# Four graph layers on one core: layer 0's row sums of score tiles, by additions on GpSimd or by accumulating DMAs

## The chip, the cores and the metric

The kernel runs on one core of a Trainium2 chip. The metric is device time in microseconds (us). The kernel before took 1689.95 us, the median of three runs (1689.92, 1689.95, 1690.58). Profiles are of one execution each.

The engines are named as the profile names them: PE is TensorE (PEld its weight loads), DVE VectorE, ACT ScalarE, POOL GpSimd, SP SyncE. SP computes nothing and issues DMAs.

## The reference

The input is a batch of 32 graphs of 512 nodes with 128 features, `x` (32 x 512 x 128), and one adjacency matrix `adj` (512 x 512) of zeros and ones. Four layers follow one another; each normalises `x`, takes the positive part as `h`, and adds its result to `x`. Layer 1 is a gated recurrent step done five times, layer 2 one multiplication by the adjacency, layer 3 three powers of it. The change is in layer 0:

```
x_h  = elu(h @ Wi + bi)
e    = sigmoid(a_tgt[:, :, None] + a_src[:, None, :] + be) * mask     # 512 x 512 scores per graph
agg  = e @ x_h
self = x_h * sum(e, axis=-1, keepdims=True)
out  = concat(elu(concat(agg, self) @ Wn + bn), x_h) @ Wm + bm
```

`mask` is the adjacency with 0.005 in place of its zeros. The sum of each row of `e`, 512 scores, is what the change computes in another way.

## The kernel before, in words

**Tiling.** Everything is held with features or nodes on the 128 partitions and 512 numbers in each, so a tile is 128 x 512 of fp32, 256 KB. A graph's scores are four such tiles, `es[0]` to `es[3]`: source nodes jc x 128 on the partitions, the 512 target nodes along the row. A row sum is thus a sum over partitions and over the four tiles. fp32 matmuls go through PE in two records each; where both operands are rounded to fp32r there is one record, and a value is then split into a rounded part and a remainder, each multiplied on its own.

**Buffers.** `Val` names a value; it takes a slot of a kind when the operation that writes it is ordered: "f" are 36 SBUF tiles of 128 x 512, "q" 4 such tiles of fp32r, "s" 8 small ones, "b" 8 PSUM banks, "m" and "d" places in DRAM. Blocks are transposed by a DVE block transpose, a DMA out to "m" (L384) and a DMA back that puts the blocks elsewhere (L395, L400, L414).

**The order of the work.** Operations of all graphs and layers are listed with `op(engine, us, due, emit, reads, writes, ...)`: an assumed duration, a due time, and `result`, the assumed delay until others see the result. `Plan.order` then runs through assumed time and picks, for each engine, the operation that is ready and due first, if its buffers are free and if it isn't due over 60 us after the oldest one left. The instructions of each engine are issued in that order, so a late operand holds up whatever stands behind it on that engine. POOL's operations and those marked `two` (DVE operations with two SBUF inputs) never overlap in the plan: a flag, `shared`, holds back one while the other runs. Steady graphs are due 56 us apart, and several graphs are in work at a time, in different layers.

The list is planned twice after a test of `adj`. Its zeros and ones are exact in fp32r, so the branch that runs is the one in which adjacency products take two fp32r passes.

**Layer 0 (`layer0`).** For each graph: x_h (L441 with Wi, then an elu of ACT and DVE operations), its products with the weights (L567), the targets' part broadcast to all partitions through DRAM (L591, L594), then for each of the four tiles a tanh on ACT (L619) and (tanh + 1) x mask on DVE (L622). L630 multiplies x_h by the four tiles into the PSUM bank `pn`. The row sums come in one of two ways:

- graphs 0 to 3 (`b < G`, G = 4): four fp32 matmuls with a matrix of ones, one per tile (L441 with ones), summed in PSUM;
- graphs 4 to 31: POOL adds the tiles, `es[0] + es[1]`, `es[2] + es[3]`, and the two sums (L641); ACT rounds the total to fp32r (L647), DVE takes the remainder (L648), and two fp32r matmuls with ones sum both over the partitions (L653).

DVE multiplies x_h by the sums (L656, `own`), L441 with Wn adds that product to `pn`, and an elu and the output product (L666) follow.

**What else is on these queues.** POOL also does one power per layernorm (L478, 128 x 4 numbers), between DVE's statistics (L476) and DVE's L481, after which ACT normalises (L486). SP issues all DMAs: graphs in and out, and the transposes.

Of the kernel before, what the change touches and what calls it, by code (L numbers as in the profile page):

```python
# [14 lines left out]
ALU = mybir.AluOpType  # L15
# [26 lines left out]
class Plan:  # L42
# [13 lines left out]
        self.pieces = {}  # L56
        self.idle = None

    def op(self, eng, us, due, emit, reads=(), writes=(), two=False, keep=0, result=None,
           earliest=0.0):  # L60

        o = Op(eng, us, self.RESULT[eng] if result is None else result, emit, two, keep)
        o.earliest = earliest
        for v in reads:
            o.before.add(v.writer)
        for v in writes:
            o.before.update(v.readers)  # L70
            if v.writer:
                o.before.add(v.writer)
            elif v.kind and v.slot is None:
                o.takes.append(v)
        for v in reads:
            v.readers.append(o)
        for v in writes:
            v.writer, v.readers = o, []
        o.vals = [v.whole or v for v in dict.fromkeys([*reads, *writes])]
        for v in o.vals:  # L80
            v.left += 1
        for v in [*reads, *writes, *o.vals]:
            self.vals[v] = True
        o.before -= {o, None}
        o.due = max([due, *(b.due for b in o.before)])
        for b in o.before:
            b.after.append(o)
        self.ops.append(o)
# [28 lines left out]
    def order(self, end=None):  # L117

        left = [o for o in self.ops if not o.begun]
        for o in reversed(left):  # L120
            o.chain = o.us + max([0.0, *(o.result + a.chain for a in o.after)])
            if end is None:
                o.due = min(o.due, self.last - o.chain)
        by_due, oldest = sorted(left, key=lambda o: o.due), 0
        coming, ready = {e: [] for e in self.until}, {e: [] for e in self.until}
        order, events, index = [], [self.now], {}
        for i, o in enumerate(left):
            index[o] = i
            o.waits = sum(not b.begun for b in o.before)
            o.ready = max([o.earliest, *(self.known(b, o) for b in o.before if b.begun)])  # L130
            if not o.waits:
                heapq.heappush(coming[o.eng], (o.ready, i, o))
                events.append(o.ready)
        events += self.until.values()
        events += [t for f in self.free.values() for t, _ in f] + [self.shared]
        events = [max(t, self.now) for t in events]
        heapq.heapify(events)

        def begins(o, now):
            if o.due > by_due[oldest].due + self.ahead:  # L140
                return False
            if (o.two or o.eng == "POOL") and self.shared > now:
                return False
            keep = 0 if o is by_due[oldest] else o.keep
            if any(v.added and self.clean(now) is None for v in o.takes):
                return False
            return all(
                len(self.free[v.kind]) > keep and self.free[v.kind][keep][0] <= now
                for v in o.takes
            )  # L150

        while events:
            now = heapq.heappop(events)
            if end is not None and now >= end:
                break
            for e in self.until:
                while coming[e] and coming[e][0][0] <= now:
                    _, i, o = heapq.heappop(coming[e])
                    heapq.heappush(ready[e], (o.due, i, o))
                if self.until[e] > now:  # L160
                    continue
                passed, o = [], None
                while ready[e] and o is None:
                    x = heapq.heappop(ready[e])
                    if begins(x[2], now):
                        o = x[2]
                    else:
                        passed.append(x)
                for x in passed:
                    heapq.heappush(ready[e], x)  # L170
                if o is not None and end is not None and any(
                    c.due < o.due and t < now + 0.3 * o.us for t, _, c in coming[e]
                ):
                    heapq.heappush(ready[e], (o.due, index[o], o))
                    o = None
                if o is None and e == "PE" and end is not None and self.idle.known <= now:
                    order.append(self.idle)
                    self.until[e] = now + self.idle.us
                    heapq.heappush(events, self.until[e])
                if o is None:  # L180
                    continue
                order.append(o)
                o.begun = True
                while oldest + 1 < len(by_due) and by_due[oldest].begun:
                    oldest += 1
                o.start, self.until[e] = now, now + o.us
                if o.two or e == "POOL":
                    self.shared = self.until[e]
                for v in o.takes:
                    v.slot = self.free[v.kind].pop(self.clean(now) if v.added else 0)[1]  # L190
                    if v.kind == "b":
                        self.pieces[v.slot] = v.pieces
                o.known = self.until[e] + o.result
                heapq.heappush(events, self.until[e])
                heapq.heappush(events, o.known)
                for v in o.vals:
                    v.left -= 1
                    if not v.left and v.kind:
                        self.free[v.kind].append((o.known, v.slot))
                        self.free[v.kind].sort()  # L200
                for a in o.after:
                    if a in index:
                        a.waits -= 1
                        a.ready = max(a.ready, self.known(o, a))
                        if not a.waits:
                            heapq.heappush(coming[a.eng], (a.ready, index[a], a))
        assert end is not None or len(order) == len(left), "the plan does not end: too few buffers"
        self.now = end or 0.0
        return order
# [3 lines left out]
def tile_four_graph_layers(  # L213
# [27 lines left out]
    nc = tc.nc  # L241
    B, N, D = x.shape
    NC = N // P
    G = 4
# [8 lines left out]
    T_VEC, T_COPY, T_ACT, T_DMA = 0.61, 0.5, 0.6, 0.45  # L253
# [3 lines left out]
    op = plan.op  # L257
# [19 lines left out]
    def at(v):  # L277
        if v.tile is not None:
            return v.tile
        return places[v.kind][v.slot] if v.whole is None else at(v.whole)[:, v.part]  # L280
# [267 lines left out]
    def layer0(b, h, due):  # L548
# [6 lines left out]
        d = due + 6  # L555
        xhT = elu(product(Wi_sb, hT, d, blocks=b >= G), bi_sb, bi_half, d, KEEP)

        d = due + 14
# [23 lines left out]
        d = due + 20  # L582
# [33 lines left out]
        es = []  # L616
        for jc in range(NC):
            e = Val("f")
            op("ACT", T_ACT, d, lambda e=e, jc=jc: nc.scalar.activation(  # L619
                like_tgt(at(e)), of_tgt(), AF.Tanh, bias=at(ends)[:, jc : jc + 1]), [tgt, ends], [e],  # L620
                keep=KEEP if jc == 0 else 0)
# [5 lines left out]
        d = due + 30  # L627
# [3 lines left out]
                at(pn), at(msg)[:, ts(jc, P)], at(es[jc]), start=jc == 0, stop=False),  # L631
                [msg, es[jc]], [pn])

        if b < G:
            ps = Val("b")
            for jc in range(NC):
                product(ones, es[jc], d, ps, start=jc == 0, stop=jc == NC - 1)
        else:
            sums = [Val("f"), Val("f")]
            def add(dst, a, c):  # L640
                op("POOL", 1.6, d - 10, lambda: nc.gpsimd.tensor_tensor(  # L641
                    at(dst), at(a), at(c), op=ALU.add), [a, c], [dst])
            add(sums[0], es[0], es[1])
            add(sums[1], es[2], es[3])
            add(sums[0], sums[0], sums[1])
            high, low, ps = Val("q"), Val("q"), Val("b")
            op("ACT", T_COPY, d, lambda: nc.scalar.copy(at(high), at(sums[0])), [sums[0]], [high])  # L647
            op("DVE", T_VEC, d, lambda: nc.vector.tensor_tensor(  # L648
                at(low), at(sums[0]), at(high).bitcast(F32), op=ALU.subtract),
                [sums[0], high], [low], two=True)  # L650
            def total():
                for n, part in enumerate((low, high)):
                    nc.tensor.matmul(at(ps), at(ones_r), at(part), start=n == 0, stop=n == 1)  # L653
            op("PE", 2 * T_PASS, d, total, [high, low, ones_r], [ps])
# [6 lines left out]
        d = due + 44  # L661
# [16 lines left out]
    def first_layer(b):  # L678
        h = layernorm(b, begin(b))
        layer0(b, h, begin(b))  # L680
# [316 lines left out]
```

## Time and profile before

| | us |
|---|---|
| median of three runs | 1689.95 |
| the profiled execution | 1689.17 |
| its span | 1687.4 |
| POOL additions L641, 84 of them | 129.9 busy, mean 1.548 |
| POOL powers L478, 128 of them | 160.0 busy, mean 1.250 |
| L622 on DVE, 128 of them | 106.2 busy, mean 0.883 (the page leaves it out; from the groups by shape) |
| L653 on PE, 56 records | 24.2 busy, mean 0.512 |
| L441 with ones on PE, 32 records | 15.2 busy, mean 0.593 |
| DMA engines, share of their time | 31.3% |

How to read it: a group's line has the kernel's line, the engine, the operation, what is written and read with its shape, the number of instructions, their busy time and mean, and the engine's idle time just before them with what ended it. Durations of matmuls overlap each other, so PE's pace is read from the chain of waits, which has no overlaps. The granted TensorE clock was 0.999 of full speed.

### The profile page before, as it was taken

To read this page: it belongs to the slowest core of one execution; us is meant where nothing else is said; L and a number is where in the kernel's file an instruction comes from. 1 tells how busy PE (TensorE), PEld (TensorE's weight loads), DVE (VectorE), ACT (ScalarE), POOL (GpSimd) and SP (SyncE) were. 2 spreads that over 40 slices of the span, in tenths; PEclk is the share of its full clock that TensorE was granted. 3 is DMA by queue.
4 is the path that set the end of the run, shared out by engine and by line. 5 is a ranking of instruction groups with operands and counts; after the bars stand their busy time and mean duration, and the time that the engine had idled before them with its cause. 6 is when DMAs were issued, how large, how long until landed. Compare 5 with 4: busy or idle time off the path is not lost.

```text
span 1687.4 us, 21306 instructions
## 1 busy us (share of the span) xinstructions
PE 1667.7 (99%) x6627; PEld 1076.8 (64%) x6627; DVE 1457.7 (86%) x3325; ACT 1127.8 (67%) x2143; POOL 295.8 (18%) x237
## 2 busy tenths in 40 slices
PE   9999999999999999999999999999999999999998
PEld 7555555656666666666666666666666666666797
DVE  6889999999998898889988898889999988877742
ACT  8777676786776676667776677665777766655541
POOL 2121102212122121222202212202222220000110
PEclk9999999999999999999999999999999999999999
DMA  3213333243333332242332433232333333222201
GB/s 107 62 57 101 94 107 94 78 135 95 101 113 101 101 101 85 84 120 95 105 103 77 112 107 92 90 107 88 118 104 99 97 98 94 82 69 88 83 18 52
DMA packets 266875, 156.57 MB, mean 93 GB/s; under 512 B 75392, under 2 KB 235008, under 8 KB 266752
## 3 DMA queue, kind: packets, MB, share of 16 engines
q1 hardware_dynamic: 266752, 155.12, 31.3%
q8 instruction: 54, 0.88, 0.2%
q14 instruction: 69, 0.57, 0.1%
HBM read 82.25 MB, written 72.81 MB: 92 GB/s over the span
## 4 chain that ended last, share of the span: by engine, by line
PE 89%; DVE 6%; ACT 2%; DMA 1%; issue 1%; SPq 0%; DVEq 0%; ACTq 0%
PE b L441 41%; PE b L820 19%; PE b L910 10%; PE b L901 6%; PE b L630 5%; PE b L666 3%; PE b L567 2%; PE b L883 1%; PE b L300 1%; DVE f L845 1%; DVE f L622 1%; DVE r L794 1%; PE b L653 1%; ACT f L486 1%; DVE f L382 1%
## 5 line engine op out<-in xcount | busy, mean ns | idle before, releaser
L478 POOL TENSOR_TENSOR s<-s,nhalf 128x4 f32<-128x4 f32 x128 | 160.0, 1250 | 884.4 <-DVE s L476 840.9
L430 ACT COPY f<-b 128x512 f32<-128x512 f32 x360 | 208.4, 586 | 158.7 <-PE b L820 107.1
L820 PE MATMUL b<-AQ,r 128*128 128x512 f32 x1024 | 302.5, 437 | 1.3 <-DVE r L794 1.3
L820 PEld LDWEIGHTS b<-AQ,r 128*128 128x128 f32 x1024 | 192.2, 188 | 89.9 <-issue 47.4
L845 DVE TENSOR_TENSOR f<-f,b 128x512 f32<-128x512 f32 x320 | 211.6, 676 | 39.8 <-PE b L441 39.1
L446 ACT ACTIVATE f<-f,b4w 128x512 f32<-128x512 f32 x160 | 115.4, 723 | 163.0 <-DVE f L845 160.5
L382 DVE STREAM_TRANSPOSE f<-f 128x512 f32<-128x512 f32 x244 | 205.2, 844 | 21.8 <-ACT f L486 21.3
L910 PE MATMUL b<-r,A_r 128*128 128x512 f32 x768 | 222.8, 426 | 0.0
L486 ACT ACTIVATE f<-x,s 128x128 f32<-128x128 f32 x512 | 210.8, 491 | 17.3 <-DVE s L481 17.2
L641 POOL TENSOR_TENSOR f<-f,f 128x512 f32<-128x512 f32 x84 | 129.9, 1548 | 427.0 <-DVE f L622 299.0
L441 PE MATMUL b<-f,u5T 128*128 128x512 f32 x320 | 163.4, 595 | 6.0 <-DVE f L852 6.0
L910 PEld LDWEIGHTS b<-r,A_r 128*128 128x128 f32 x768 | 139.4, 189 | 46.6 <-issue 24.4
L441 PE MATMUL b<-f,w4T 128*128 128x512 f32 x320 | 163.1, 593 | 2.5 <-ACT f L430 2.5
L441 PE MATMUL b<-f,u3T 128*128 128x512 f32 x320 | 163.3, 593 | 1.7 <-DVE f L866 1.6
L441 PE MATMUL b<-f,w5T 128*128 128x512 f32 x320 | 162.5, 592 | 0.0
L441 PE MATMUL b<-f,w3T 128*128 128x512 f32 x320 | 162.1, 592 | 0.0
L820 PE MATMUL b<-A_r,r 128*128 128x512 f32 x512 | 151.1, 437 | 0.4 <-DVE r L794 0.4
L901 PEld LDWEIGHTS b<-V,f 128*128 128x128 f32 x1024 | 131.8, 191 | 26.3 <-issue 20.1
L862 DVE TENSOR_TENSOR f<-f,f 128x512 f32<-128x512 f32 x160 | 112.9, 707 | 38.0 <-ACT f L446 37.7
L446 ACT ACTIVATE f<-b,b5w 128x512 f32<-128x512 f32 x160 | 109.1, 683 | 53.3 <-PE b L441 52.9
L794 DVE TENSOR_TENSOR r<-f,r 128x512 fp32r<-128x512 f32 x192 | 138.5, 723 | 6.4 <-ACT r L790 6.2
L446 ACT ACTIVATE f<-f,b3w 128x512 f32<-128x512 f32 x160 | 115.0, 720 | 28.8 <-DVE f L845 27.7
(106 smaller groups left out, 2580.5 us busy)
## 6 DMA issues: line engine op xcount, KB each, us to landing
m<-f SPq DMA_DIRECT2D x244, 256.0 KB, 2.1
f<-m SPq DMA_DIRECT2D x184, 256.0 KB, 2.9
f<-m SPq DMA_DIRECT2D x240, 64.0 KB, 2.3
x<-in_x_dram SPq DMA_DIRECT2D x32, 256.0 KB, 3.3
out_dram<-x SPq DMA_DIRECT2D x32, 256.0 KB, 2.4
f<-d SPq DMA_DIRECT2D x28, 256.0 KB, 5.6
f<-in_adj_dram SPq DMA_DIRECT2D x4, 256.0 KB, 3.8
f<-in_L_gnn_weight_dram SPq DMA_DIRECT2D x2, 224.0 KB, 3.3
```

The lines of the kernel that those rows point to most:

```text
L382: op("DVE", us, due, lambda: nc.vector.transpose(view_out(at(blocks)), view_in(at(src))), [src], [blocks])
L430: op("ACT", us, due, lambda: nc.scalar.copy(at(t), at(src)), [src], [t])
L441: nc.tensor.matmul(to, at(w), of, start=start, stop=stop)
L446: op("ACT", us, due, lambda: nc.scalar.activation(at(dst), at(src), AF.Tanh, bias=at(bias), scale=scale), [src, bias], [dst])
L478: op("POOL", 1.35, due, lambda: nc.gpsimd.tensor_tensor(stat(SCALE), stat(VAR), at(neg_half), op=ALU.pow), [s, neg_half], [s])
L486: nc.scalar.activation(at(h)[:, ts(c, P)], at(X[b])[:, c, :], AF.Relu, bias=stat(SHIFT)[:, c : c + 1], scale=stat(SCALE)[:, c : c + 1],)
L641: op("POOL", 1.6, d - 10, lambda: nc.gpsimd.tensor_tensor(at(dst), at(a), at(c), op=ALU.add), [a, c], [dst])
L794: op("DVE", T_VEC, due, lambda: nc.vector.tensor_tensor(part(lo), whole(), part(hi).bitcast(F32), op=ALU.subtract), [src, hi], [lo], two=two)
L820: nc.tensor.matmul(at(pa), at(part)[:, ts(jc, P)], view(at(columns)[:, jc, :]), start=jc == n == 0, stop=jc == NC - 1 and n == PARTS - 1,)
L845: op("DVE", T_VEC, d, lambda: nc.vector.tensor_tensor(at(s), at(u), at(pg), op=ALU.add), [u, pg], [s])
L901: nc.tensor.matmul(at(pz)[:, ts(i, D)], at(hT[i])[:, ts(ic, P)], at(V[k]), start=i == 0, stop=last and i == G - 1,)
L910: nc.tensor.matmul(at(pz), at(adjT)[:, jc, ts(ic, P)], at(part), start=False, stop=jc == NC - 1 and n == PARTS - 1,)
```

## The change

Graphs 2 and 3 sum as graphs 4 to 31 do. And for all of these the four tiles are added otherwise: SP copies `es[0]` to the buffer `sums[0]`, SBUF to SBUF, and POOL issues three DMAs that add `es[1]`, `es[2]` and `es[3]` to it, each after the one before has landed. One "f" buffer is taken in place of two. The plan is told 0.45 us and a delay of 2.6 for the copy, 1.0 us and 3.0 for each accumulating DMA (1.6 and 0.2 for an addition before), and that these DMAs may overlap `two` operations. Since the plan changes, the order of the instructions of all engines changes. With one line more near the top, lines after it are numbered higher by one; in the changed kernel the copy is L641 and the accumulating DMAs are L644.

```diff
-    def op(self, eng, us, due, emit, reads=(), writes=(), two=False, keep=0, result=None,
+    def op(self, eng, us, due, emit, reads=(), writes=(), two=None, keep=0, result=None,
            earliest=0.0):
+        two = eng == "POOL" if two is None else two
         o = Op(eng, us, self.RESULT[eng] if result is None else result, emit, two, keep)
...
-            if (o.two or o.eng == "POOL") and self.shared > now:
+            if o.two and self.shared > now:
...
-                if o.two or e == "POOL":
+                if o.two:
                     self.shared = self.until[e]
...
-        if b < G:
+        if b < 2:
             ps = Val("b")
             for jc in range(NC):
                 product(ones, es[jc], d, ps, start=jc == 0, stop=jc == NC - 1)
         else:
-            sums = [Val("f"), Val("f")]
-            def add(dst, a, c):
-                op("POOL", 1.6, d - 10, lambda: nc.gpsimd.tensor_tensor(
-                    at(dst), at(a), at(c), op=ALU.add), [a, c], [dst])
-            add(sums[0], es[0], es[1])
-            add(sums[1], es[2], es[3])
-            add(sums[0], sums[0], sums[1])
+            sums = [Val("f")]
+            op("SP", T_DMA, d - 10, lambda: nc.sync.dma_start(at(sums[0]), at(es[0])),
+               [es[0]], [sums[0]], result=2.6)
+            for e in es[1:]:
+                op("POOL", 1.0, d - 10, lambda e=e: nc.gpsimd.dma_start(
+                    at(sums[0]), at(e), accum_op=ALU.add), [e, sums[0]], [sums[0]],
+                   two=False, result=3.0)
             high, low, ps = Val("q"), Val("q"), Val("b")
```

## The prediction

> **What bounds the kernel now.** I read the page's busy shares first, then its slices, then the stretches table, and last the timeline around one graph's sum.
>
> ```profile
> PE 1667.7 (99%) x6627; PEld 1076.8 (64%) x6627; DVE 1457.7 (86%) x3325; ACT 1127.8 (67%) x2143; POOL 295.8 (18%) x237
> PE   9999999999999999999999999999999999999998
> DVE  6889999999998898889988898889999988877742
> L641 POOL TENSOR_TENSOR f<-f,f 128x512 f32<-128x512 f32 x84 | 129.9, 1548 | 427.0 <-DVE f L622 299.0
> m<-f SPq DMA_DIRECT2D x244, 256.0 KB, 2.1
> ```
>
> PE is busy in every slice. As a busy PE can be padded by modelled ends, I added its work up at the pace at which the chain of waits steps through it: 0.43 us for each record of an fp32 512-wide matmul, two records per matmul, and 0.23 us for a fp32r one. Over the instruction order that gives 1658 us for a span of 1687.4. So PE is really full; about 20 us are start, end and stalls. POOL is idle four fifths of the time, and removing its work does not by itself shorten anything.
>
> ```profile
> 692.78 0.47 PE b L653 x2
> 693.24 2.58 PE b L441 x6
> ```
>
> These two steps of the chain are the prices: 2.58 / 6 = 0.43 and 0.47 / 2 = 0.235.
>
> ```profile
> 336.00:504.00 168.00, 165.61 (x646) 105.09 (x645) 165.28 (x394) 124.91 (x245) 35.29 (x26) 1.00 0.38 110
> 504.00:1134.00 630.00, 627.53 (x2482) 406.38 (x2481) 557.53 (x1268) 426.52 (x810) 117.58 (x84) 1.00 0.34 98
> ```
>
> The columns are length, then busy time of PE, PEld, DVE, ACT, POOL, then clock, DMA share, GB/s. In the first stretch DVE is as full as PE (165.3 of 168) and PE loses 2.4 us; in the second DVE has 11% to spare.
>
> ```profile
> 680.09 3.59 DVE L622 SCALAR_TENSOR_TENSOR f<-f,mask 128x512 f32<-128x512 f32 x4
> 681.53 1.60 POOL L641 TENSOR_TENSOR f<-f,f 128x512 f32<-128x512 f32 x1 [24.57 <-DVE f L622]
> 683.76 3.03 POOL L641 TENSOR_TENSOR f<-f,f 128x512 f32<-128x512 f32 x2 [0.63 <-DVE f L622]
> 688.84 0.62 ACT L647 CAST q<-f 128x512 fp32r<-128x512 f32 x1
> 690.25 0.68 DVE L648 TENSOR_TENSOR q<-f,q 128x512 fp32r<-128x512 f32 x1
> ```
>
> This is one graph's sum. The four score tiles are done from 680.8 to 683.7, the sums at 686.8; ACT rounds at 688.8, DVE subtracts at 690.25, and PE adds up (L653) at 692.2. Nobody waits long: the order is written so that each step comes just after its operand.
>
> **What the Trainium skill says.** "SBUF — State Buffer", section "SBUF: two separate sides": a DVE instruction with two SBUF inputs and a GpSimd instruction that reads SBUF take turns on one port pair, the loser blocks. The trace agrees: three of these four L622 took 0.69 us and the one that met a POOL addition 1.75; over the run L622 has a mean of 883 ns against that 692, and L641 spreads from 1257 to 4007 ns. "DMA: Bandwidth & Descriptors", section "Two DMAs through the same engine are not ordered": the issuer of a dependent DMA has to wait on the first one's semaphore; the instruction order shows these waits on POOL. The price comes from the same page, section "Anatomy of one DMA — SWDGE (gpsimd) path": about 2.0 us + bytes / 436e3 per GpSimd DMA. No GpSimd DMA is in the trace of before.
>
> **The change part by part.** The sum is made against the profiled execution, 1689.17 us (span 1687.4 and 1.8 around it); the median of 1689.95 is 0.78 above.
>
> *Graphs 2 and 3 leave the matmul with ones.* Two graphs lose four fp32 matmuls (L441 with ones) each and get two fp32r ones (L653): 2 x (4 x 0.86 - 2 x 0.235) = 2 x 2.97 = 5.94 us of PE less. Adding up the changed order at the same prices gives the same, 1658.1 to 1652.2. PE is full also where they lie (before 126 us it idles 1.7 us), so the saving moves all that follows: -5.9. ACT gets 2 x 0.62 and DVE 2 x 0.69 more, over two graphs in which ACT and DVE have 20% to spare: nothing; on PE's path it would be 2.6.
>
> *84 POOL additions go.* POOL's 129.9 us cost nothing where they stood. What they cost is the blocked DVE: 128 x (883 - 692) ns = 24 us of DVE. That only counts where DVE is the limit, in the stretch 336 to 504, where PE lost 2.4 us in all. Bounds 0 and -2.4; I take -1.0.
>
> *30 copies on SP.* Each is one issue of 0.34 us, 10 us in a queue that mostly waits for DVE. It waits for the first score tile, and the block copies of other graphs (L384, L395, L414) are queued behind it; the tile is made by the DVE instruction just before, so nothing: without that cover, the 0.7 us of one L622. Landing: as m<-f, 2.1 us.
>
> *90 accumulating DMAs on POOL, three in a row per graph.* Each waits for the landing of the one before, so three links in series stand where 5.2 us of additions stood. What does a link cost, from wait to landing? From below: a plain copy of this size by SP lands in 2.1. From above: the slowest 256 KB row of the page, f<-d, 5.6. The price of the skill's page gives 2.0 + 0.6 = 2.6 for a plain one, as an estimate. An accumulation reads its destination too: 8 packets of 2 KB per engine at 88 ns (the mean of such packets in this trace) are another 0.7. With 0.3 for the start after a wait I take 3.6.
>
> What is the cover? In the changed order I added up PE's work between the end of a graph's last L630 and its L653: median 13.6 us, against 8.0 before, so the order itself was stretched. The first tile was done 3.7 us before that end in the timeline above. From first tile to L653 there are thus 17.3 us. Needed: copy 2.1 + 3 links + rounding, subtraction and their semaphores 1.8. With 3.6 this is 14.7: hidden, with 2.6 us to spare. PE starts to wait at (17.3 - 3.9) / 3 = 4.5 per link. ACT, which is in order, reaches L647 some 4.5 us before L653 by the PSUM tiles that it reads just before; it starts to wait at (17.3 - 4.5 - 2.1) / 3 = 3.6, exactly my value, and between 3.6 and 4.5 its waiting delays the tanh and copies behind it, which have a microsecond or two of room. So 0 here, but on the edge.
>
> *POOL's queue.* 27 layernorm powers (L478) stand between a graph's first and last sum instruction, against 6 before. Each is queued behind a wait for a landing, and DVE's L481, then ACT's L486, wait for it. At 3.6 the landing is no later than the order allows: 0; if a link is 1 us later, that microsecond goes to DVE's queue in 27 places.
>
> *DMA engines.* 30 copies at 0.7 and 90 accumulations at 1.4 us of all 16 engines are 147 us, on top of the 31.3% of the span: 40%. Late landings get more likely. The chain shows two now (7.8 us m<-f at 257.7, 7.3 us f<-d at 1133.4), in stretches where PE lost 2.6 and 1.5 us. I add one more of that kind: +2.0 (bounds 0 and +10).
>
> Sum: 1689.17 - 5.9 - 1.0 + 2.0 = 1684.2; with 0.78 for the median, **1685.0**.
>
> **Rivals.** *The links are longer than the cover (slower).* At 5.0 us per link the sum is late by 2.1 + 15 + 1.8 - 17.3 = 1.6 us in each of 30 graphs: 48 us, less the 5.9: 1732. It decides from 4.5 on; break-even is at 30 x (3L - 13.4) = 5.9, L = 4.53. At the upper bound of 5.6 it is 30 x 3.4 = 102 us: 1786. For it: three serial round trips, an accumulation that no row shows, ACT already at its edge at 3.6. Against it: SP's copies land in 2.1, and the order leaves 5.6 us more than before.
>
> *The gain is eaten (no change).* Three or four late landings of 1.5 to 2 us each, or powers that come late in POOL's queue, give back the 5.9: 1690. For it: the two late ones of today at 31% DMA share. Against: most of their latency is hidden.
>
> *The change saves no PE time.* If PE had nothing to pull forward in the first 100 us, it would idle where the ones stood: 1690 too. The slices speak against it: PE is full from the start.
>
> **How the numbers follow.** Links within the cover: 0.50, 1685 (1680 to 1688). Gain eaten or not realised: 0.15, 1690. Links over the cover: 0.35, from 1695 to 1786, in the middle 1732. About 0.2% (3.4 us) is what a measurement can tell from no change: below 1686.6 is faster, above 1693.3 slower. Of the first case a little ends within that, of the last too: faster 0.49, same 0.15, slower 0.36. Range: 0.05 lie below 1680 and 0.13 above 1735. The likeliest case's own range is 1680 to 1688.
>
> **What would show it.** Right: PE records of L653 x60 and of ones x16; L622's mean near 0.7 us; an accumulation that lands within 4 us; ACT's idle before the rounding small; PE idle some 15 us in 1680. Wrong: ACT's rounding waiting for a DMA by microseconds per graph, then DVE's subtraction and PE's L653; or L481 waiting for POOL's power; then the links are what I mis-sized.

## The result and the profile after

The changed kernel takes 1678.94 us (median of four runs, 1677.93 to 1680.66) against 1690.18 before (a fourth run added to the three above): a ratio of 0.9936 with a 95% interval of 0.9922 to 0.9949, 11.2 us less. The prediction said 1685.0 with a range from 1680: the direction was right, but the gain is more than twice what was forecast and the time falls below the range. The profiled execution took 1678.16, with a span of 1676.4.

Its page, the lines that answer to those shown of before:

```profile
PE 1662.9 (99%) x6615; PEld 1073.7 (64%) x6615; DVE 1420.3 (85%) x3327; ACT 1130.5 (67%) x2145; POOL 239.6 (14%) x243
PE   9999999999999999999999999999999999999998
DVE  6888999999988888889888898888999988877742
L644 POOL DMA_DIRECT2D f<-f x90 | 80.7, 896 | 536.4 <-DVE f L865 58.1
f<-f POOLq DMA_DIRECT2D x90, 256.0 KB, 3.6
f<-f SPq DMA_DIRECT2D x30, 256.0 KB, 2.3
```

PE's busy time fell by 4.8 us, its idle time (span less busy) from 19.7 to 13.5, and DVE's busy time by 37.4. An accumulating DMA occupies POOL for 0.9 us and lands 3.6 us after its issue; 3.6 was what I had taken for a whole link. The same two stretches, same columns as before:

```profile
336.00:504.00 168.00, 167.43 (x646) 105.96 (x645) 155.07 (x376) 124.10 (x241) 25.55 (x25) 1.00 0.44 123
504.00:1134.00 630.00, 627.99 (x2478) 404.88 (x2477) 546.63 (x1274) 425.38 (x804) 91.39 (x86) 1.00 0.44 119
```

DVE is no longer full in the first of them, and PE loses 0.6 us there in place of 2.4. One graph's sum in the timeline:

```profile
667.40 2.53 DVE L623 SCALAR_TENSOR_TENSOR f<-f,mask 128x512 f32<-128x512 f32 x4 [1.00 <-ACT f L620]
668.12 0.50 SPq L641 DMA_DIRECT2D f<-f  x1
671.10 0.92 POOL L644 DMA_DIRECT2D f<-f  x1 [12.91 <-DMA f<-f]
675.29 0.90 POOL L644 DMA_DIRECT2D f<-f  x1
679.35 0.86 POOL L644 DMA_DIRECT2D f<-f  x1 [3.16 <-DMA f<-f]
683.13 0.62 ACT L648 CAST q<-f 128x512 fp32r<-128x512 f32 x1 [0.93 <-DMA f<-f]
684.42 0.68 DVE L649 TENSOR_TENSOR q<-f,q 128x512 fp32r<-128x512 f32 x1
```

The four mask products take 2.53 us, not 3.59: none of them is lengthened. The copy is issued at 668.12 and its landing lets POOL start 3.0 us later; then the links follow at distances of 4.19, 4.06 and, from the last issue to ACT's rounding, 3.78 us; ACT waits 0.93 us for it. The sum is ready 15 us after the first tile. The 60 distances from one issue to the next in the same graph have a median of 4.13 us (3.8 to 5.3).

### The profile page after: what moved, and what is told of

The parts are those of the page before. It is cut to its first block, busy times and chain, and to the rows that moved or that the text cites. A ratio compares the mean times of both kernels' runs of the same rounds, so it can differ in the third digit from the quotient of the medians.

```text
span 1676.4 us, 21509 instructions
## 1 busy us (share of the span) xinstructions
PE 1662.9 (99%) x6615; PEld 1073.7 (64%) x6615; DVE 1420.3 (85%) x3327; ACT 1130.5 (67%) x2145; POOL 239.6 (14%) x243
## 3 DMA queue, kind: packets, MB, share of 16 engines
q1 hardware_dynamic: 271072, 162.98, 32.5%
## 4 chain that ended last, share of the span: by engine, by line
PE 62%; DMA 2%; DVE 1%; ACT 0%; issue 0%; SPq 0%; DVEq 0%; POOLq 0%
PE b L442 27%; PE b L821 13%; PE b L911 9%; PE b L902 5%; PE b L631 3%; PE b L667 2%; PE b L884 1%; DMA f<-f 1%; PE b L568 1%; DMA m<-f 1%; PE b L654 1%; DMA f<-m 0%; DVE f L383 0%; SPq L420 0%; ACT f L620 0%
## 5 line engine op out<-in xcount | busy, mean ns | idle before, releaser
L479 POOL TENSOR_TENSOR s<-s,nhalf 128x4 f32<-128x4 f32 x128 | 154.8, 1212 | 822.0 <-DVE s L477 702.6
L442 PE MATMUL b<-f,u5T 128*128 128x512 f32 x320 | 163.3, 593 | 1.0 <-DVE f L853 1.0
L442 PE MATMUL b<-f,u3T 128*128 128x512 f32 x320 | 163.3, 593 | 1.0 <-DMA f<-m 1.0
L442 PE MATMUL b<-f,w4T 128*128 128x512 f32 x320 | 162.8, 592 | 0.0
L442 PE MATMUL b<-f,w3T 128*128 128x512 f32 x320 | 162.4, 592 | 0.0
L442 PE MATMUL b<-f,w5T 128*128 128x512 f32 x320 | 162.4, 592 | 0.0
L644 POOL DMA_DIRECT2D f<-f x90 | 80.7, 896 | 536.4 <-DVE f L865 58.1
L863 DVE TENSOR_TENSOR f<-f,f 128x512 f32<-128x512 f32 x160 | 109.2, 683 | 48.9 <-ACT f L447 48.4
L447 ACT ACTIVATE f<-f,b3w 128x512 f32<-128x512 f32 x160 | 114.9, 719 | 43.1 <-DVE f L846 42.2
L795 DVE TENSOR_TENSOR r<-f,r 128x512 fp32r<-128x512 f32 x192 | 130.5, 682 | 12.6 <-ACT r L791 12.4
```

Source lines behind the costliest of these rows:

```text
L442: nc.tensor.matmul(to, at(w), of, start=start, stop=stop)
L447: op("ACT", us, due, lambda: nc.scalar.activation(at(dst), at(src), AF.Tanh, bias=at(bias), scale=scale), [src, bias], [dst])
L479: op("POOL", 1.35, due, lambda: nc.gpsimd.tensor_tensor(stat(SCALE), stat(VAR), at(neg_half), op=ALU.pow), [s, neg_half], [s])
L795: op("DVE", T_VEC, due, lambda: nc.vector.tensor_tensor(part(lo), whole(), part(hi).bitcast(F32), op=ALU.subtract), [src, hi], [lo], two=two)
L863: op("DVE", T_VEC, d, lambda c=c, h=h: nc.vector.tensor_tensor(at(c), at(c), at(h), op=ALU.subtract), [c, h], [c], two=True)
```

## The experiments

Two theories for the 6 us or so that PE's saving doesn't explain: A, DVE is no longer blocked by GpSimd's reads, and I had priced this too low; B, the new order of instructions is better. Fourteen kernels were run, in four sets, each beside the kernel before, which took between 1689.21 and 1689.64 in them.

| kernel | us | ratio to before [95%] |
|---|---|---|
| two graphs only, by additions | 1685.91 | 0.9978 [0.9969, 0.9987] |
| DMAs only, from the fifth graph | 1679.87 | 0.9948 [0.9934, 0.9961] |
| new order, additions | 1694.57 | 1.0030 [1.0019, 1.0041] |
| old order, memsets | 1677.38 | 0.9927 [0.9913, 0.9940] |
| four links | 1809.79 | 1.0711 [1.0692, 1.0729] |
| tree | 1690.99 | 1.0011 [1.0004, 1.0017] |
| old order, one copy | 1678.92 | 0.9937 [0.9924, 0.9950] |
| tree from the fifth graph | 1700.57 | 1.0067 [1.0054, 1.0080] |
| plan told 4.4 us a link | 1677.62 | 0.9926 [0.9912, 0.9939] |
| the same, from the fifth graph | 1682.40 | 0.9952 [0.9939, 0.9966] |
| plan told 4.8 us a link | 1670.94 | 0.9890 [0.9875, 0.9905] |
| tree, plan told its delays | 1670.82 | 0.9885 [0.9870, 0.9901] |
| old order, halved additions | 1686.36 | 0.9985 [0.9977, 0.9992] |
| old order, two copies | 1682.21 | 0.9959 [0.9945, 0.9972] |

**One part of the change alone.** First the two graphs without DMAs:

```diff
-        if b < G:
+        if b < 2:
```

> The kernel before with one edit: graphs 2 and 3 also go by GpSimd additions and two fp32r matmuls; nothing by DMA. PE's work falls by the 5.94 us of the prediction. If that saving is passed on in full and the rest of the measured 11.2 us comes from the DMAs, this takes 1684 us (1682.5 to 1686). If the saving in the first 100 us is lost because PE has nothing to pull forward, it stays at 1690. If the two graphs alone are the whole gain, it takes 1679.

Measured: 1685.91, 3.7 us less. The saving arrives for the larger part; the same edit also adds six GpSimd additions, and DVE's busy time grew by 11 us. The profiled execution (1687.40, one of the slower ones) also lost time in the first 100 us to a granted clock of 0.50 for 3.4 us, of which more below.

Then the DMAs without the two graphs (in the changed kernel):

```diff
-        if b < 2:
+        if b < G:
```

> The changed kernel with graphs 0 to 3 left on the matmul with ones, so only the other edit: copy and accumulating DMAs for graphs 4 to 31. No PE work is saved. Both theories of the extra gain, DVE no longer blocked by GpSimd's reads or a better order, expect about 5 us off: 1685 us (1683 to 1687). If the DMAs bring nothing, 1690.

Measured: 1679.87, 9.8 us less with no PE work saved. So nearly the whole gain is in the DMAs, which had been predicted to bring +1.0 (less blocking 1.0, late landings 2.0). It is about twice what either theory had set down (1683 to 1687).

**Order or reads?** Two kernels keep an order exactly and change only who reads. New order, additions again:

```diff
-                op("POOL", 1.0, d - 10, lambda e=e: nc.gpsimd.dma_start(
-                    at(sums[0]), at(e), accum_op=ALU.add), [e, sums[0]], [sums[0]],
+                op("POOL", 1.0, d - 10, lambda e=e: nc.gpsimd.tensor_tensor(
+                    at(sums[0]), at(sums[0]), at(e), op=ALU.add), [e, sums[0]], [sums[0]],
```

> The changed kernel with its instruction order kept on all engines, but each accumulating DMA is a GpSimd addition of the same tiles in the same place (sums plus tile, 90 of them). Only the unit that adds differs. Theory A, DVE blocked by GpSimd's reads: the block comes back, DVE's mask products take 0.85 us or more again, and the time rises to 1683 to 1686. Theory B, the new order makes the gain: within 1 us of 1679, or below it, since three additions of 1.6 us end sooner than three links of 3.6.

Old order, nothing read:

```diff
-                op("POOL", 1.6, d - 10, lambda: nc.gpsimd.tensor_tensor(
-                    at(dst), at(a), at(c), op=ALU.add), [a, c], [dst])
+                op("POOL", 1.6, d - 10, lambda: nc.gpsimd.memset(
+                    at(dst), 300.0), [a, c], [dst])
```

> The kernel before with its instruction order kept on all engines, but each of the 84 GpSimd additions is a memset of the same destination, which reads nothing; this leaves out the sum over the four tiles (the row sums are of a constant). Theory A: DVE is no longer blocked, its mask products take 0.69 us, DVE's busy time falls by 30 us or more and the time falls by about 5 us, to 1685. Theory B: the order is the old one, so the time stays within 1.5 us of 1690.

Measured: 1694.57, that is 15.6 us above the changed kernel in the very same order, and 1677.38, that is 12.3 us below the kernel before in its own. Theory B isn't needed: the old order without reads gains at least as much as the whole change does, although PE has 5.94 us more work in it, so the new order, with its late links, is no better than the old. A holds, at more than twice the size that I expected. The 15.6 us may overstate it, as the new order was planned with the additions free to overlap DVE's operations of two SBUF inputs, which the old plan keeps apart; the new order with memsets, which would show the order alone, was not run. Nor is it the shorter time of POOL that helps: with additions ACT's rounding waits 0.5 us for POOL's sums in the whole run, and DVE waits 1.4 us for its powers with additions and with memsets alike; and two copies in that place, below, keep POOL busy for longer than an addition and cost less. The page of the new order with additions, then of the old order with memsets:

```profile
PE 1667.8 (99%) x6615; PEld 1074.0 (63%) x6615; DVE 1472.9 (87%) x3327; ACT 1130.4 (67%) x2145; POOL 299.3 (18%) x243
```

```profile
PE 1665.6 (99%) x6627; PEld 1078.3 (64%) x6627; DVE 1412.1 (84%) x3325; ACT 1130.5 (67%) x2143; POOL 206.7 (12%) x237
```

DVE's busy time differs by 52.6 us from the changed kernel and by 45.6 from the kernel before, with the same DVE instructions. The memsets show something else: they write as much as the additions and don't lengthen DVE's operations. Where the blocked time went is seen in groups by shape. Before:

```profile
L622 DVE SCALAR_TENSOR_TENSOR f<-f,mask 128x512 f32<-128x512 f32 x128 | 106.2, 883 | 4.5 <-ACT f L619 4.4
L794 DVE TENSOR_TENSOR r<-f,r 128x512 fp32r<-128x512 f32 x192 | 138.5, 723 | 6.4 <-ACT r L790 6.2
```

and the same with memsets:

```profile
L622 DVE SCALAR_TENSOR_TENSOR f<-f,mask 128x512 f32<-128x512 f32 x128 | 81.6, 691 | 3.8 <-ACT f L619 3.8
L794 DVE TENSOR_TENSOR r<-f,r 128x512 fp32r<-128x512 f32 x192 | 131.0, 684 | 8.8 <-ACT r L790 8.6
```

L622 gives 24.6 us, L794 7.5, and the four groups of the recurrent step's operations (L852, L862, L864, L866) another 12; together they are 44 of the 45.6 us. And PE waits for such a result. Who waited for whom (us, times, longest), before and then with memsets:

```profile
PEld b L441 <- DVE f L852: 14.2, 22, 2.6
PE b L441 <- DVE f L852: 6.0, 5, 1.8
```

```profile
PEld b L441 <- DVE f L852: 3.3, 9, 1.1
PE b L441 <- DVE f L852: 0.7, 1, 0.7
```

L852 is one of the recurrent step's operations, in another layer than the sums. PE's idle time falls from 19.7 to 10.9 us, and 5.3 us of that are at this one place.

**What a block costs.** A GpSimd copy in that place reads one tile and lasts 0.96 us:

```diff
-                op("POOL", 1.6, d - 10, lambda: nc.gpsimd.tensor_tensor(
-                    at(dst), at(a), at(c), op=ALU.add), [a, c], [dst])
+                op("POOL", 1.6, d - 10, lambda: nc.gpsimd.tensor_copy(
+                    at(dst), at(a)), [a, c], [dst])
```

> The kernel before with its order kept, but each GpSimd addition is a GpSimd copy of its first operand: one tile read in place of two, one written. The sum over the tiles is left out. With a memset in that place (no read) the time was 1677.4, with the addition 1689.6. If any GpSimd read blocks DVE for as long as the instruction lasts, the cost goes by the copy's duration: 1682 to 1686 if it lasts 0.6 to 0.9 us. If only reads of two tiles block: 1677 to 1678.

Measured: 1678.92, hardly more than without reads, though DVE's busy time is 20.8 us higher than with memsets and L622 takes 769 ns: a read of one tile does block, but costs little. Neither case had set that down. This left open what the cost goes by, and two more runs in the old order were to tell length of block from total of reading, in place of the same two lines:

```diff
...
+                op("POOL", 1.6, d - 10, lambda: [nc.gpsimd.tensor_tensor(
+                    at(dst)[:, ts(n, 256)], at(a)[:, ts(n, 256)], at(c)[:, ts(n, 256)],
+                    op=ALU.add) for n in range(2)], [a, c], [dst])
```

> The kernel before with its order, each GpSimd addition cut in two of 256 columns; the sums are the same. GpSimd reads as long in total or longer, but an instruction that gets the ports holds them for some 0.8 us in place of 1.55. Theory C, the price goes by the length of one block: most of the 12.2 us go, 1679 to 1683. Theory D, it goes by the total of GpSimd's reading: 1688 to 1692.

```diff
...
+                op("POOL", 1.6, d - 10, lambda: [nc.gpsimd.tensor_copy(
+                    at(dst), at(x)) for x in (a, c)], [a, c], [dst])
```

> The kernel before with its order, each GpSimd addition replaced by two GpSimd copies, of its first and of its second operand, into the same destination; the sum over the tiles is left out. GpSimd's reading time is double that of the single copy (1678.9 us), about 160 us, with blocks of 0.96 us. Theory C: 1679 to 1682. Theory D: DVE's busy time rises by another 20 us, to that of the additions, and so does the time: 1686 to 1690.

Measured: 1686.36 and 1682.21. Neither theory fits: halved additions (0.98 us each) keep three quarters of the cost (2.9 us below before), and two copies read longer in total (147 us) than additions (130) and cost less. What does order all five is DVE's busy time, and the cost grows faster than it:

| in the place of an addition | POOL busy there | DVE busy | us |
|---|---|---|---|
| memset | 42.2 | 1412.1 | 1677.38 |
| copy | 78.9 | 1432.9 | 1678.92 |
| two copies | 147.4 | 1448.1 | 1682.21 |
| halved additions | 159.5 | 1451.3 | 1686.36 |
| addition (before) | 129.9 | 1457.7 | about 1689.5 |

The first 21 us of blocking cost 1.5 us, the next 15 cost 3.3, the last 10 cost some 7. It looks like slack that is used up, but that is an inference from five points.

**How close the chain is to its limit.** The slower rival of the prediction was tested with one more link, in a planned order that doesn't know of it:

```diff
...
+                    if last:
+                        nc.gpsimd.dma_start(at(sums[0]), at(mask)[:, 0, :], accum_op=ALU.add)
```

> The changed kernel with its planned order, but after each graph's third accumulating DMA a fourth one adds a tile of the mask to the same sums, unknown to the plan; the row sums are thus of other numbers. In the changed kernel a link takes 4.1 us from one issue to the next and copy, three links, rounding and subtraction about 17 us, against the 17.3 us of cover of the prediction. If that cover is right and every microsecond over it is PE's loss, a fourth link costs 3.8 to 4.1 us in each of 30 graphs: 1790 to 1802 us. If there is more slack than counted, half of it or less: under 1740. If the chain is far inside its cover: within 2 us of 1679.

Measured: 1809.79, 131 us more and over the range. Its waits, longest in total first:

```profile
ACT q L650 <- DMA f<-mask: 146.7, 30, 9.1
DVE q L651 <- ACT q L650: 116.1, 28, 7.4
```

That is 4.4 us for each of 30 graphs and looks like the length of a link, but it is made of two parts. PE's idle time grows by 85.5 us (99.0 against 13.5), 2.85 us for each graph, so about a third of a link was absorbed. The other 45 us are PE's busy time (1707.9 against 1662.9), for the same matmuls: the mean granted clock is 0.974, where it was 0.999 before. PE stopped for L656 from 630.4 to 635.2, and the clock followed (columns as before, the clock third from the end):

```profile
630.00:635.00 5.00, 0.36 (x2) 0.00 (x0) 0.53 (x1) 1.18 (x3) 0.78 (x1) 0.80 0.65 130
635.00:639.00 4.00, 3.78 (x12) 3.08 (x13) 4.00 (x9) 1.61 (x3) 0.00 (x0) 0.50 0.01 4
```

The clock was 0.50 from 633.0 to 639.8; two records of L442 took 1.92 us at 637.94 and 1.02 at 640.61. There are 21 such stretches of 3.4 or 6.8 us in this run before PE's end, 92 us in all, and at half the clock PE gets half as much done in them: 46 us as an estimate. In the traces of all sixteen kernels there are 29, and each begins 2.1 to 5.1 us after the start of a pause of PE of 1.8 to 6.5 us. Every pause over 2.6 us was followed by one, none under 1.8. So a long stall of PE costs more than its length; neither the prediction nor this run's expectation had that.

The cover comes out at 18 to 19 us, a little over the 17.3. In the traces the first score tile is done 4.5 us before the end of the last L630 (median before), not 3.7, which gives 18.1, and from first tile to L654 the changed kernel takes 18.7 (median of 30 graphs). Its chain, 17 to 18 us, nearly uses this up.

**A shorter chain.** A tree of two links in series:

```diff
-            sums = [Val("f")]
-            op("SP", T_DMA, d - 10, lambda: nc.sync.dma_start(at(sums[0]), at(es[0])),
-               [es[0]], [sums[0]], result=2.6)
-            for e in es[1:]:
-                op("POOL", 1.0, d - 10, lambda e=e: nc.gpsimd.dma_start(
-                    at(sums[0]), at(e), accum_op=ALU.add), [e, sums[0]], [sums[0]],
+            sums = [Val("f"), Val("f")]
+            for s, e in zip(sums, (es[0], es[2])):
+                op("SP", T_DMA, d - 10, lambda s=s, e=e: nc.sync.dma_start(at(s), at(e)),
+                   [e], [s], result=2.6)
+            for s, e in ((sums[0], es[1]), (sums[1], es[3]), sums):
+                op("POOL", 1.0, d - 10, lambda s=s, e=e: nc.gpsimd.dma_start(
+                    at(s), at(e), accum_op=ALU.add), [e, s], [s],
```

> The changed kernel with the sum as a tree: SP copies the first and the third tile, GpSimd's DMAs add the second and the fourth to these copies, and one more adds the two: as many accumulating DMAs, one copy and one buffer more, but two links in series in place of three, with the plan told of it. If ACT's waits for the sums (29.9 us over 19 graphs) reach PE, this gains: 1675 to 1678. If they are absorbed: 1678 to 1680. If the extra DMA traffic or buffer costs: above 1680.

and with graphs 0 to 3 left on the matmul with ones:

> The tree, with graphs 0 to 3 on the matmul with ones. The chain of DMAs gained only 0.9 us from graphs 2 and 3 (1679.9 against 1678.9), where PE's work falls by 5.94. If their sums come too late in the first 100 us because of the long chain, the tree restores the difference: this is 4 to 6 us slower than the tree from the third graph on. If PE's work saved there is lost for another reason, the two trees differ by 0 to 2 us.

Measured: 1690.99 and 1700.57, a miss: 12 us slower than the chain, and with graphs 0 to 3 on the ones another 10, more than the 4 to 6 expected. The tree's DMA rows and waits:

```profile
f<-f POOLq DMA_DIRECT2D x90, 256.0 KB, 3.9
f<-f SPq DMA_DIRECT2D x60, 256.0 KB, 2.9
```

```profile
ACT q L649 <- DMA f<-f: 46.2, 20, 5.1
DVE q L650 <- ACT q L649: 27.9, 17, 3.3
PEld b L655 <- DVE q L650: 20.2, 17, 3.3
PE b L655 <- DVE q L650: 10.3, 9, 2.4
```

A copy lands at 2.9 us, not 2.3, an accumulation at 3.9. Of the two accumulations of a pair, issued 1.3 us apart, the first lands after 3.6 and the second after 4.3 (medians), and the third is issued 6.1 us after the first, where the plan was told 5.0. The plan shortened the cover along with the chain, so the delay went through ACT and DVE to PE: 10.3 us of PE's idle time are at L655, and three stretches of half clock add some 5 us.

**The plan told the truth.** The same kernels with other assumed delays and nothing else:

```diff
-                   two=False, result=3.0)
+                   two=False, result=3.4)
```

> The changed kernel with one number: the plan is told a delay of 3.4 us in place of 3.0 after an accumulating DMA, so 4.4 a link where 4.0 was told and 4.13 (median, 3.8 to 5.3) measured. The same work, another order. If ACT's 29.9 us of waiting for the sums reach PE, they shrink to under 12 us and the time falls to 1674 to 1677. If they are absorbed: 1678 to 1680.

with graphs 0 to 3 on the matmul with ones:

> The kernel with 4.4 us told per link, and graphs 0 to 3 on the matmul with ones. If graphs 2 and 3 gave only 0.9 of their 5.94 us because late sums stalled what followed, then with a plan that knows the delay the two graphs give 4 us or more: this takes 1679 to 1682 where the one from the third graph on takes 1674 to 1677. If a stall in the first 100 us takes the saving whatever is planned, the two differ by less than 2 us.

with `result=3.8`:

> As the kernel with 4.4 us told per link, but with 4.8, which covers five in six of the measured links. ACT hardly waits for sums (under 6 us in all). If what is left of the stalls comes from late links, it is another 0 to 2 us faster than with 4.4. If tiles held longer cost more, it is slower than with 4.4 by up to 4 us.

and the tree with 3.4 for its copies and 3.8 for its accumulations:

> The tree of two links with the delays that it showed on the chip: a copy lands later beside its twin (2.9 us, told 3.85 with its issue) and an accumulation too (3.9, told 4.8). Only the plan's numbers change against the tree before (1691.0). If that tree was slow because its plan was told too little and each microsecond over came out of PE, this takes 1674 to 1679. If the extra copies and buffers themselves cost the 12 us, it stays at 1688 or more.

Measured: 1677.62, 1682.40, 1670.94, 1670.82. The first two end just over their ranges, and the last two below what was expected (0 to 2 us under the first, and 1674 to 1679). They are the fastest of the study, 18.7 and 18.8 us below their kernel before and 8 us below the changed kernel. The tree gained 20 us by two numbers of its plan, so its transfers were not what made it slow. Its copies now land at 2.4 us, though the two of a pair are as close as before (1.2 us apart, median): a twin alone doesn't make a copy late. ACT's wait for the sums was 29.9 us in the changed kernel and is 8.8, 13.8, 9.1 and 9.0 in these four:

```profile
ACT q L648 <- DMA f<-f: 29.9, 19, 4.9
```

```profile
ACT q L648 <- DMA f<-f: 9.1, 8, 2.7
```

(the changed kernel, and the one with 4.8 us a link). With 4.4 the wait shrank as much, but the time only by 1.3 us. Its chain of waits shows another stall, in the stretch from 308 to 336, where PE was busy 23.7 of 28 us, and its clock the price of it:

```profile
316.69 3.52 DMA m<-f
321.21 4.63 ACT f L487 x12
```

```profile
329.00:335.00 6.00, 5.40 (x19) 4.36 (x20) 3.59 (x6) 4.79 (x10) 0.70 (x1) 0.50 0.75 199
```

These are a block transpose and three layernorms in a row, not the sums; PE's longest wait there is 4.2 us, and then the clock is 0.50 for 6.8 us, a loss of 3.4 more by estimate. Together they are nearly the whole difference between the profiled executions with 4.4 and with 4.8 (7.7 us of span: 4.4 of PE's idle time, 3.3 of its busy time). The order from the fifth graph has such a one too, a landing of f<-m after 7.16 us, and two stretches of half clock. A new order deals such stalls anew, so differences of 2 to 4 us between two orders can't be put on one edit.

## Why the prediction was wrong

- *PE's work, -5.9: the work is right, that all of it arrives isn't shown.* L654 has 60 records and ones 16, as said. Alone it gave 3.7 with additions; between the two orders planned with 4.4 us it gives 4.8, but both have a stall of their own. Between the DMAs alone and the changed kernel it is 0.9, and why is open: late sums of graphs 2 and 3 are not it, as in the first 130 us ACT waits only 1.1 us for sums. How much of it arrives differs with the order, from 0.9 to 4.8 us.
- *DVE's blocking, -1.0 with bounds 0 and -2.4: this is the step that failed.* The same order without reads is 12.3 us faster. Two errors in it. I counted only L622 (24 us), where DVE's busy time falls by 45.6 in all. And I counted DVE's time only in the stretch where its busy share is full, and bounded it by PE's idle time in that one. That stretch hardly gains: PE lost 2.4 us in it and still loses 1.9 without the reads. The gain is in the others, where DVE is 91 or 94% busy and PE waits for its results all the same. Before:

```profile
84.00:168.00 84.00, 82.33 (x282) 47.81 (x281) 76.13 (x149) 60.71 (x112) 18.12 (x13) 1.00 0.26 79
168.00:336.00 168.00, 164.15 (x541) 94.13 (x540) 157.91 (x344) 116.17 (x215) 29.39 (x21) 1.00 0.30 93
```

and without the reads:

```profile
84.00:168.00 84.00, 84.00 (x288) 49.03 (x287) 73.20 (x154) 63.09 (x115) 8.16 (x10) 1.00 0.26 82
168.00:336.00 168.00, 166.77 (x563) 97.15 (x561) 153.25 (x349) 119.85 (x225) 19.17 (x21) 1.00 0.31 93
```

  PE lost 5.5 us in these two and loses 1.2. Over the first 1660 us it lost 13.6 and loses 4.9; with the 2.1 us by which its busy time falls that is the difference of the two spans, 10.9. A bound that holds here is PE's whole idle time of about 13 us in place of the 2.4 of one stretch.
- *The links, 0 on the edge: half right.* My 3.6 for a whole link is the landing alone; the next link begins 4.13 after the last. The copy takes 3.0 to its successor's start, not 2.1. Needed were thus 3.0 + 3 x 4.13 + 1.8 = 17.2 us, not 14.7. The cover was mis-sized too, and the other way: the 3.7 in it should have been 4.4 in the timeline shown there (first tile at 680.8, last L630 ends at 685.2), so some 18 us. That this second error made up for part of the first was luck. There was about 1 us of room, where I had 2.6. What this edge costs was hidden under the larger gain: the order that allows for it is 8.0 us faster.
- *POOL's queue, 0: right.* DVE's L482 waits 3.3 us for the powers in all (1.4 before).
- *DMA engines, 40% of their time: right* (32.5 + 8.5 = 41%). *One more late landing, +2.0:* not seen as a loss against before in the changed kernel; other orders show stalls of this kind, and where one stops PE for over 2.6 us, a stretch of half clock followed.

Put together from the runs: -12.3 for the reads and -5.9 for PE's work make 1671.4 of 1689.6, which is within 0.6 us of the kernel planned with 4.8 us a link; the changed kernel takes 7 to 8 more. Late sums are a part of that, but only 2.8 us of PE's idle time there are at L654; the rest isn't shown to be theirs. The terms come from different orders and the 5.9 didn't arrive in full in any pair of runs, so that the sum fits is in part luck.

## What to carry to other kernels

Before pricing work that is taken off a shared resource, bound the gain by all of the bound engine's idle time and by every instruction that can meet it, not by the one stretch or group where the collision is visible. Where an order is planned from assumed delays, measure the distance from issue to issue of the new operation and tell the plan a value near its upper end: 0.8 us more a link came with 8 us here (0.4 more with only 1.3, as that order had a stall elsewhere), and a shorter chain with too small a number lost 12. Where an edit makes the bound engine wait for microseconds, read its granted clock too, as the wait may cost half as much again. To split a result into order and mechanism, keep each order and change only what its instructions do.

## What the runs showed of the hardware

After each pause of PE of over 2.6 us, and some of 1.8 to 2.6, the granted clock was 0.50 for 3.4 or 6.8 us, and PE's work took up to twice as long: with four links 21 times, 45 us of 131.

A GpSimd memset of 128x512 (0.53 us) didn't slow DVE's operations with two SBUF inputs (L622 at 691 ns, 688 in the changed kernel), while a GpSimd copy that reads one tile did (769 ns); so it is GpSimd's reading that collides, one tile or two. Accumulating DMAs of 256 KB issued by GpSimd between SBUF tiles landed in 3.2 to 4.9 us in the changed kernel, and their issues (0.85 to 1.1 us on POOL) left DVE's times alone too. Their packets of 2 KB took 195 ns, those of other queues 88. A plain copy between SBUF tiles landed in 2.3 us (median), in 2.9 in the first tree and in 2.4 in the tree whose plan was told its delays.
